# A fused two-layer convolution kernel: gate and NCA in batches of 32 rows, the gate's products over 2 sources x 6 rows in the lattice's column order, NCA's part of two blocks at once

## The chip, the cores and the metric

The kernel runs on one core of a Trainium2 chip. A core has five engines that run beside each other, each with its own instruction stream: TensorE (PE, matmuls, with its weight loads listed as PEld), VectorE (DVE), ScalarE (ACT), GpSimd (POOL) and SyncE (SP), which here issues nearly all DMAs. TensorE's array has 128 x 128 cells; a matmul may use half or a quarter of its columns (or half of its rows), and matmuls on different parts can run side by side. The metric is device time in microseconds (us), from runs of the whole program; the profile is of one execution.

## The reference, cut to what matters

The input is 32 images of 8 channels, 256 x 256, float32. Layer 0 normalises each pair of channels (`_gn`) and then computes three things and mixes them:

```python
drive = x[:, :C_OUT]; grid = drive
for _ in range(STEPS):                       # 15 steps: the lattice (CML)
    mapped = R * grid * (1.0 - grid)
    local = _conv(mapped, K_local, groups=C_OUT)          # 3x3, per channel
    physics = (1.0 - EPS) * mapped + EPS * local
    grid = (1.0 - BETA) * physics + BETA * drive
cml_out = jnp.clip(grid, 0.0001, 1.0 - 0.0001)
h = jax.nn.relu(_conv(x, Wp, bp))            # NCA: 3x3, 8 -> 128
nca_out = jax.nn.sigmoid(_conv(h, Wu, bu))   # 1x1, 128 -> 8
gin = jnp.concatenate([x, cml_out, nca_out], axis=1)      # 24 channels
g = jax.nn.sigmoid(_conv(jax.nn.relu(_conv(gin, Wg1, bg1)), Wg2, bg2))  # gate: 3x3, 24 -> 8; 1x1, 8 -> 8
return g * cml_out + (1.0 - g) * nca_out
```

Here `x` is the normalised input; the layer's result is added to the input. Layer 1 normalises that sum, quantises it with one scale over all images, convolves it (3x3, 8 to 8) and adds again.

## The kernel before, in words

The kernel has two stages. The first is layer 0 for all images, the second layer 1. The images go in 8 groups (NG) of 4 (GB). Work passes between the parts through scratch in HBM: `xp_s` (normalised input in rows with padding, as a high and a low part), `xq_s` (normalised input with its columns sorted into four phases, column 4j+q at place 64q+j), `cm_s` (CML, in the same column order), `nc_s` (NCA, plain columns) and `y_s` (layer 0's result). `xp_s`, `xq_s`, `cm_s` and `nc_s` have 12 buffers of an image each (NBUF).

Four parts share the engines in the first stage.

- *prep* (`normalise`): takes jobs of one image and one or two channel pairs, has the statistics summed by two small matmuls (L330, L359), and stores to `xq_s` and `xp_s`.
- *lattice*: 8 channels x 15 steps a group. A step has three tiles of columns; each tile runs six matmuls (L511), in array halves, for two halves of the group (`jobs`), then two VectorE operations each (L519, L524). After a step, rows at tile borders are exchanged by DMAs on SP (`exchange`, L474 and L475). `background` (L464) spreads the loads of the next channel and the stores of the last over the steps, three DMAs a tile.
- *nca*: `rows` (L569) loads windows of 48 partitions (6 rows of 8 values: three input rows, high and low part) for 28 rows of an image in two parts. `hidden` (L591) runs pairs of matmuls in two halves of the array's rows, ScalarE applies Relu (L601), and `place` (L608) sums 128 hidden values to 8 outputs with matmuls of 32 array columns, up to four side by side. A tenth batch has the last 4 rows.
- *gate*: 9 batches of 28 rows and one of 4, an image. A batch is two blocks of 16 rows x 8 channels on 128 partitions, which overlap by two rows, since a block of 16 rows gives 14. `stage` loads `nb`, `cq` and `xb` (the raw input) with DMAs on SP. `arrange` puts CML's columns back in order on GpSimd (L723), normalises `xb` on VectorE into `xnb` (L729), and forms `d` and `f` on GpSimd. Then 9 matmuls in two array halves (L795), three sources x three column shifts, 512 columns each, then Relu (L812), the second matmul (`pg`, L758), Sigmoid (L760), mix and statistics (L762 to L773), and a store.

The order of TensorE's instructions is the order in which the program writes them (`manual_schedule`). It is set by generators: `lattice` is the main one; `together` lets it do a step (it yields 5.91) and then takes pieces from the filler until the filler's share done equals the lattice's. The filler is made by `both` from nca of the group, gate of the group before, and prep of the next. The shares are reckoned with `T_NCA, T_GATE, T_PREP, T_LATTICE` (L916) and with the numbers that the generators yield, which are the author's guesses of a piece's time. The gate of the last group runs after the last lattice, alone. SP issues its DMAs in the program's order too, and an issue that waits holds all behind it.

In the second stage (from L936) `yb` is loaded from `y_s`, quantised, convolved and stored, image by image.

Of the kernel before, what the change touches and what calls it, by code (L numbers as in the profile page):

```python
# [40 lines left out]
P = 128  # L41
C = 8
# [11 lines left out]
ROW = 2 * C * PW  # L54
R4 = 32
# [12 lines left out]
K_M, K_A, K_B, K_MASK, K_JUNK, K_GRP = 0, 384, 512, 640, 644, 646  # L68
K_COLS = 650


def _constants():
# [5 lines left out]
    n = 2 * H * W  # L78
    same = (c[:, None] // 2) == (c[None, :] // 2)
    mask_a = (r >= 1) & (r <= 14)  # L80
    mask_b = (r >= 1) & (r <= 4)
    k[:, K_A : K_A + P] = same * mask_a[:, None] * (18.0 * W / n)
    k[:, K_B : K_B + P] = same * mask_b[:, None] * (1.0 * W / n)
    k[:, K_MASK + 0] = mask_a
    k[:, K_MASK + 1] = mask_b
    k[:, K_MASK + 2] = r >= 1
    k[:, K_MASK + 3] = r <= 4
# [26 lines left out]
def kernel(  # L114
# [26 lines left out]
    masks = cp.tile([P, 4], F32, name="masks")  # L141
    sel_a = cp.tile([P, P], F32, name="sel_a")
    sel_b = cp.tile([P, P], F32, name="sel_b")
# [7 lines left out]
    gw = cp.tile([P, 9, P], F32, name="gw")  # L151
# [16 lines left out]
    xq_s = [dp.tile([C, H, 4, NJ], F32, name=f"xq_s{i}") for i in range(NBUF)]  # L168
    cm_s = [dp.tile([PROWS, C, W], F32, name=f"cm_s{i}") for i in range(NBUF)]
    nc_s = [dp.tile([PROWS, C, W], F32, name=f"nc_s{i}") for i in range(NBUF)]  # L170
    y_s = [dp.tile([PROWS, C, W], F32, name=f"y_s{b}") for b in range(B)]

    with tc.tile_pool(name="prep", bufs=1) as pp, tc.tile_pool(name="prep2", bufs=2) as pp2:
# [5 lines left out]
        g1 = pp.tile([P, 216], F32, name="g1")  # L179
        nc.sync.dma_start(g1, wg1)  # L180
# [17 lines left out]
        for t, n, w in (  # L198
            *((t, 2 * C, PW) for t in xp_s),
            *((t, C, W) for t in (*nc_s[:GB], *cm_s[:GB], *nc_s[GB:], *cm_s[GB:], *y_s)),  # L200
        ):
            k = 64 if w == W else 43
            for row, m in ((0, 1), (257, 5), (262, 5), (267, 1)):
                borders.append(
                    (
                        dram_ap(t, row * n * w, [[w, m * n], [k, w // k], [1, k]]),
                        zt[: m * n, :k].unsqueeze(1).to_broadcast([m * n, w // k, k]),
                    )
                )
        for _ in range(4 * GB):  # L210
            nc.scalar.dma_start(*borders.pop(0))

        V.tensor_copy(masks, kt[:, K_MASK : K_MASK + 4])
        V.tensor_copy(junk, kt[:, K_JUNK : K_JUNK + 2])
        V.tensor_copy(grp, kt[:, K_GRP : K_GRP + 4])
        V.tensor_copy(sel_a, kt[:, K_A : K_A + P])
        V.tensor_copy(sel_b, kt[:, K_B : K_B + P])
# [22 lines left out]
        for s in range(3):  # L240
            for dx in range(3):
                blocks(gw[:, s * 3 + dx, :], g1, lambda dy: ((s * 3 + dy) * 3 + dx) * C)
# [23 lines left out]
    with ExitStack() as one:  # L266
# [7 lines left out]
        hp, xp, sp2, gp, bp2 = pool("hp", 12), pool("xp", 4), pool("sp2", 1), pool("gp", 3), pool("bp2", 2)  # L274
        st, imp, wk, wk1, np_ = pool("st", 2), pool("imp", 3), pool("wk", 2), pool("wk1", 2), pool("np", 1)
        ps_c, ps_a = pool("ps_c", 6, space=PSUM), pool("ps_a", 2, space=PSUM)
# [3 lines left out]
        xnbs = [fixed([P, 2, PW], f"xnb{i}") for i in range(2)]  # L280
        cmbs = [fixed([P, 2, PW], f"cmb{i}") for i in range(3)]
        nbs = [fixed([P, 2, PW], f"nb{i}") for i in range(3)]
# [3 lines left out]
        for t in (*xnbs, *cmbs, *nbs):  # L286
            for w in (0, PW - 1):
                G.memset(t[:, :, w], 0.0)
# [12 lines left out]
        def normalise(jobs):  # L301
# [36 lines left out]
            def stores(b, g, xq):  # L338
                for h in range(2):
                    nc.sync.dma_start(  # L340
                        dram_ap(xq_s[b % NBUF], (2 * g * H + P * h) * W, [[W, P], [H * W, 2], [1, W]]),
# [54 lines left out]
        def lattice(g):  # L396


            def load(u):
# [4 lines left out]
                for s in range(2):  # L404
                    i = (2 * u + s) % 4
                    da, db = d_a[i], d_b[i]
                    for k in range(2):
                        src = xq_s[((u // C) * GB + 2 * s + k) % NBUF]
                        ts = slice(NT * k, NT * k + NT)
                        for i in range(8):  # L410
                            q, odd = divmod(i, 2)
                            dims = [[2 * W, 16], [TSTEP * W, NT], [1, NJ]]
# [168 lines left out]
        def nca(b):  # L581
# [85 lines left out]
            if done:  # L667
                nc.sync.dma_start(*done)
# [427 lines left out]
```

## Time and profile before

| | |
|---|---|
| time before, median of 3 runs | 13897.23 us (13894.44 to 13898.17) |
| span of the profiled execution | 13862.1 us |
| median less that span | 35.1 us |
| instructions | 229831 |
| granted TensorE clock, mean | 0.975 |
| DMA packets | 2287210, 1496.77 MB, mean 108 GB/s |
| lattice matmuls (L511) | 2 x 17280 instructions |
| nca matmuls (L591; L608) | 2 x 12288; 8320 |
| gate matmuls (L795; L758) | 3 x 3840; 1280 |
| first lattice matmul, last | 86 us, 12930 us |
| last gate matmul | 13291 us |

The profile gives, for every engine, when each instruction ran. "Busy" is the time in which an engine ran anything; a busy TensorE is not TensorE at its peak, since its matmuls are pipelined and overlap. What a stream of matmuls costs is read from the distance between starts. The chain of waits follows the program back from its last instruction, at each step to what released it, so that its shares say what the span was spent on. A float32 matmul shows as two instructions (two passes), each with a weight load. Group 0's lattice has nca but no gate beside it, groups 1 to 7 have both.

### The profile page before, as it was taken

Reading aid. Unit: us, or ns where it says so; the run is one execution under the profiler, and the core shown is the slowest. Engines: PE = TensorE matmul, PEld = TensorE weight load, DVE = VectorE, ACT = ScalarE, POOL = GpSimd, SP = SyncE. Lnnn points to the kernel's source line nnn. Section 1 sums busy time; section 2 is a strip of 40 time slices with the busy share of each in tenths; the row PEclk is TensorE's granted clock in tenths of the full one; section 3 lists DMA queues with packets and bytes.
Section 4 is the critical chain, followed back from the end, with each engine's and each line's share of the span. In section 5 each row is a group of like instructions: output and inputs, shape, how many; then the busy total and the mean of one; then the engine's idle time right before and its main releaser. Section 6 shows DMA issues by size and latency. Waiting matters only on the chain.

```text
span 13862.1 us, 229831 instructions
## 1 busy us (share of the span) xinstructions
PE 13134.4 (95%) x81840; PEld 6403.4 (46%) x81840; DVE 8176.8 (59%) x16402; ACT 4028.2 (29%) x6274; POOL 2454.7 (18%) x4278
## 2 busy tenths in 40 slices
PE   4899999999999999999999999999999999999964
PEld 2445544444444444444444444444444444444322
DVE  5555565566655565555655565555655555555577
ACT  2233223232322223322323223222223222222123
POOL 1001111121111211111111111112111111111310
PEclk8999999999999999999999999999999999999986
DMA  6444444444444444444444444444444433333368
GB/s 152 96 97 99 96 104 112 101 98 101 111 99 103 109 93 108 108 104 93 107 106 101 102 104 103 102 106 108 94 108 110 100 91 84 89 79 89 90 202 257
DMA packets 2287210, 1496.77 MB, mean 108 GB/s; under 512 B 1096576, under 2 KB 2257152, under 8 KB 2285952
## 3 DMA queue, kind: packets, MB, share of 16 engines
q1 hardware_dynamic: 2191360, 1392.13, 43.1%
q10 hardware_dynamic: 94720, 89.93, 2.1%
q8 instruction: 665, 10.90, 0.3%
q14 instruction: 465, 3.81, 0.1%
HBM read 866.48 MB, written 478.69 MB: 97 GB/s over the span
## 4 chain that ended last, share of the span: by engine, by line
PE 81%; DMA 8%; SPq 4%; DVE 3%; issue 1%; ACTq 1%; ACT 0%; POOL 0%; POOLq 0%; DVEq 0%
PE pt L511 36%; PE ph L591 20%; PE pa L795 16%; PE acc L608 7%; DMA yb<-y_s 2%; PE pg L758 2%; DMA im<-xp_s 1%; DVE gt L519 1%; ACTq L1021 1%; DMA m_a<-m_a 1%; DMA xb<-in_x_dram 1%; DMA xp_s<-lo 1%; SPq L464 1%; SPq L569 1%; DVE m_a L524 1%
## 5 line engine op out<-in xcount | busy, mean ns | idle before, releaser
L511 PE MATMUL pt<-m_a,lw 128*64 128x390 f32 x17280 | 5842.6, 496 | 162.0 <-DMA m_a<-m_a 103.3
L511 PE MATMUL pt<-m_b,lw 128*64 128x384 f32 x17280 | 5809.7, 491 | 18.9 <-DVE m_b L430 18.1
L601 ACT ACTIVATE h<-ph,bp_sb 128x512 f32<-128x512 f32 x4096 | 2581.8, 684 | 4845.8 <-PE ph L591 4772.4
L511 PEld LDWEIGHTS pt<-m_a,lw 128*64 128x64 f32 x17280 | 2302.2, 138 | 1795.4 <-issue 1597.2
L511 PEld LDWEIGHTS pt<-m_b,lw 128*64 128x64 f32 x17280 | 2310.1, 138 | 1638.4 <-issue 1522.3
L591 PE MATMUL ph<-im,wp_hi 48*128 48x512 f32 x12288 | 2685.1, 415 | 119.0 <-DMA im<-xp_s 59.4
L519 DVE SCALAR_TENSOR_TENSOR gt<-pt,d_b 128x390 f32<-128x390 f32 x2880 | 1609.3, 559 | 1820.8 <-PE pt L511 1818.2
L519 DVE SCALAR_TENSOR_TENSOR gt<-pt,d_a 128x384 f32<-128x384 f32 x2880 | 1584.1, 550 | 1837.4 <-PE pt L511 1836.7
L591 PE MATMUL ph<-im,wp_lo 48*128 48x512 f32 x12288 | 2569.9, 398 | 0.0
L528 POOL TENSOR_TENSOR m_b<-m_b,junk 128x12 f32<-128x12 f32 x2688 | 817.1, 304 | 8414.1 <-DVE m_b L524 7988.0
L591 PEld LDWEIGHTS ph<-im,wp_hi 48*128 48x128 f32 x12288 | 1312.0, 187 | 969.7 <-DVE m_a L524 180.7
L524 DVE SCALAR_TENSOR_TENSOR m_b<-gt 128x390 f32<-128x390 f32 x2688 | 1557.1, 579 | 46.4 <-DVE gt L519 0.9
L524 DVE SCALAR_TENSOR_TENSOR m_a<-gt 128x384 f32<-128x384 f32 x2688 | 1540.3, 573 | 18.0
L591 PEld LDWEIGHTS ph<-im,wp_lo 48*128 48x128 f32 x12288 | 1309.2, 188 | 218.6
L608 PE MATMUL acc<-h,wu_z 128*32 128x512 f32 x8320 | 1155.1, 598 | 6.1 <-ACT nca L626 5.5
L795 PE MATMUL pa<-cmb,gw 128*64 128x512 f32 (+1 forms) x3840 | 861.4, 580 | 15.5 <-POOL cmb L723 15.5
L795 PE MATMUL pa<-xnb,gw 128*64 128x512 f32 (+1 forms) x3840 | 847.8, 574 | 11.1 <-ACT r L812 11.1
L795 PE MATMUL pa<-nb,gw 128*64 128x512 f32 (+1 forms) x3840 | 847.2, 573 | 0.0
L762 DVE TENSOR_TENSOR gate<-gate,d 128x512 f32<-128x512 f32 x320 | 218.3, 682 | 823.0 <-ACT gate L760 805.0
L812 ACT ACTIVATE r<-pa,bv 128x512 f32<-128x512 f32 x320 | 213.1, 666 | 1650.4 <-PE pa L795 1650.4
L729 DVE TENSOR_SCALAR xnb<-xb,sc 128x256 f32<-128x256 f32 x608 | 305.0, 517 | 596.9 <-DMA xb<-in_x_dram 590.7
L760 ACT ACTIVATE gate<-pg,bv 128x512 f32<-128x512 f32 x320 | 213.2, 666 | 1519.1 <-PE pg L758 1508.1
(133 smaller groups left out, 7225.3 us busy)
## 6 DMA issues: line engine op xcount, KB each, us to landing
im<-xp_s SPq DMA_DIRECT2D x1152, 193.5 KB
im<-xp_s SPq DMA_DIRECT2D x1216, 96.8 KB
d_a<-xq_s SPq DMA_DIRECT2D x2048, 36.0 KB
nb<-nc_s SPq DMA_DIRECT2D x288, 256.0 KB
cq<-cm_s SPq DMA_DIRECT2D x288, 256.0 KB
xb<-in_x_dram SPq DMA_DIRECT2D x544, 128.0 KB
yb<-y_s ACTq DMA_DIRECT2D x28, 2432.0 KB
xp_s<-hi SPq DMA_DIRECT2D x256, 258.0 KB
```

What stands on the lines that cost most here:

```text
L511: T.matmul(pt[half], lw[:, c, k, half], beside if part == 2 else own, start=part < 2, stop=part > 0,)
L519: V.scalar_tensor_tensor(gt, pt, FLOOR, d[:, ts, :], ALU.max, ALU.add)
L524: V.scalar_tensor_tensor(to, gt, 1.0, gt, ALU.subtract, ALU.mult)
L528: G.tensor_tensor(edge, edge, junk.unsqueeze(1).to_broadcast([P, 6, 2]), ALU.mult)
L591: T.matmul(ph[:, :n].rearrange("p (h w) -> p h w", w=W), w[64 * i : 64 * i + 48, dx, :], rhs[:, :, dx : dx + W], start=(dx == 0 and w is w ...
L601: S.activation(h[:, :n], ph[:, :n], AF.Relu, bias=bp_sb)
L608: T.matmul(acc[32 * g : 32 * g + 32, :cols], wu_z[:, 24 - 8 * i : 56 - 8 * i], h, start=first, stop=last,)
L729: V.tensor_scalar(xnb[:, k, 1 : 1 + W], xb[:, k, :], sc[:, i : i + 1], sc[:, 1:2], ALU.subtract, ALU.mult,)
L758: T.matmul(pg[half, :cols], gw2[:, half], r1[:, :cols], start=True, stop=True)
L760: S.activation(gt[:, :cols], pg[:, :cols], AF.Sigmoid, bias=bv[:, 1:2])
L762: V.tensor_tensor(three(y), three(gt), d[:, :n, :], ALU.mult)
L795: T.matmul(three[half], gw[:, s * 3 + dx, half], t[:, :n, dx : dx + W], start=(i == 0), stop=(i == 8),)
```

## The change

Gate and nca now work in 8 batches of 32 rows, an image, with nothing left over. All three sources of the gate lie in one scratch tensor `gs_s` of three parts (normalised input, CML, NCA), all in the lattice's column order; `xq_s` goes, and the lattice loads from part 0. NCA's Sigmoid (ScalarE) writes its columns in that order. The gate loads `gin` (96 partitions: 6 rows x 8 channels of the normalised input and of CML; 8 blocks of 4 output rows), `gnc` (96 partitions: twice 6 rows of NCA, for two blocks) and `mix` (the three sources at the output rows). A block of 4 rows gives 32 outputs, so one matmul over `gin` has 32 array columns, and one over `gnc` 64. A column shift in the sorted order is a move by 64 places, except at a phase border, so each shift but the middle one falls into two pieces (`PARTS`).

```diff
-    xq_s = [dp.tile([C, H, 4, NJ], F32, name=f"xq_s{i}") for i in range(NBUF)]
-    cm_s = [dp.tile([PROWS, C, W], F32, name=f"cm_s{i}") for i in range(NBUF)]
-    nc_s = [dp.tile([PROWS, C, W], F32, name=f"nc_s{i}") for i in range(NBUF)]
+    gs_s = [dp.tile([3, PROWS, C, W], F32, name=f"gs_s{i}") for i in range(NBUF)]
...
-        for _ in range(4 * GB):
+        for _ in range(2 * NBUF):
             nc.scalar.dma_start(*borders.pop(0))
...
-        hp, xp, sp2, gp, bp2 = pool("hp", 12), pool("xp", 4), pool("sp2", 1), pool("gp", 3), pool("bp2", 2)
-        st, imp, wk, wk1, np_ = pool("st", 2), pool("imp", 3), pool("wk", 2), pool("wk1", 2), pool("np", 1)
-        ps_c, ps_a = pool("ps_c", 6, space=PSUM), pool("ps_a", 2, space=PSUM)
+        hp, xp, sp2, gp, gip = pool("hp", 8), pool("xp", 3), pool("sp2", 1), pool("gp", 3), pool("gip", 2)
+        st, imp, wk, np_ = pool("st", 2), pool("imp", 2), pool("wk", 2), pool("np", 1)
+        ps_c, ps_a = pool("ps_c", 6, space=PSUM), pool("ps_a", 1, space=PSUM)
...
+        def rows(b, t):
+
+            im = imp.tile([P, 2, 8, PW], F32R, name="im", tag="im")
+            for k in range(2):
                 for q in range(2):
                     nc.sync.dma_start(
+                        im.bitcast(F32)[64 * q : 64 * q + 48, k],
+                        dram_ap(
+                            xp_s[b % NBUF], (32 * t + 16 * k + 8 * q) * ROW, [[PW, 48], [ROW, 8], [1, PW]]
+                        ),
                     )
...
+            def drain():
+                acc, t, i, hs = pend
+                for g in range(4):
+                    T.matmul(
+                        acc[32 * g : 32 * g + 32], wu_z[:, 24 - 8 * i : 56 - 8 * i], hs[4 * g + i],
+                        start=(i == 0), stop=(i == 3),
+                    )
...
+            for t in range(NT8):
+                im = ahead
+                acc = ps_a.tile([P, 512], F32, name="acc", tag="acc")
+                for i in range(4):
                     hs = {}
+                    for n in (i, i + 4):
+                        hs[n], hs[n + 8] = hidden([im[64 * q : 64 * q + 48, :, n, :] for q in range(2)])
+                    if i == 2:
...
+                        if t < NT8 - 1:
+                            ahead = rows(b, t + 1)
...
+                    if pend:
+                        done = drain() or done
+                    pend = (acc, t, i, hs)
+                    yield 3.7
...
+        def stage(b, t):
+
+            src = gs_s[b % NBUF]
+            gin = gip.tile([96, 8, W], F32, name="gin", tag="gin")
+            for j in range(2):
                 nc.sync.dma_start(
+                    gin[48 * j : 48 * j + 48],
+                    dram_ap(src, j * PART + 32 * t * C * W, [[W, 48], [4 * C * W, 8], [1, W]]),
                 )
+            gnc = gip.tile([96, 4, W], F32, name="gnc", tag="gnc")
+            for h in range(2):
+                nc.sync.dma_start(
+                    gnc[48 * h : 48 * h + 48],
+                    dram_ap(src, 2 * PART + (32 * t + 4 * h) * C * W, [[W, 48], [8 * C * W, 4], [1, W]]),
                 )
+            mix = gip.tile([P, 3, 2, W], F32, name="mix", tag="mix")
+            for k in range(2):
+                nc.sync.dma_start(
+                    mix[:, :, k, :],
+                    dram_ap(src, (32 * t + 16 * k + 1) * C * W, [[W, P], [PART, 3], [1, W]]),
                 )
...
+        def arrange(sc, mix):
+
+            d = wk.tile([P, 512], F32, name="d", tag="d", bufs=1)
+            f = wk.tile([P, 512], F32, name="f", tag="f", bufs=1)
+            G.tensor_tensor(d, flat(mix[:, 1]), flat(mix[:, 2]), ALU.subtract)
+            S.activation(f, flat(mix[:, 0]), AF.Identity, bias=sc[:, 0:1], scale=sc[:, 2:3])
+            G.tensor_tensor(f, f, flat(mix[:, 2]), ALU.add)
+            return d, f
...
+        PARTS = (
+            (1, slice(0, 256), slice(0, 256)),
+            (0, slice(64, 256), slice(0, 192)),
+            (0, slice(1, 64), slice(192, 255)),
+            (2, slice(0, 192), slice(64, 256)),
+            (2, slice(192, 255), slice(1, 64)),
+        )
...
+            for t in range(NT8):
+                gin, gnc, mix = ahead
+                pa = ps_a.tile([P, 512], F32, name="pa", tag="pa")
+                three = pa.rearrange("p (k w) -> p k w", w=W)
+                for n, (dx, to, of) in enumerate(PARTS):
+                    for i in range(4):
+                        T.matmul(
+                            three[32 * i : 32 * i + 32, :, to], gw[:, dx, :32], gin[:, i::4, of],
+                            start=(n == 0), stop=False,
+                        )
+                if last:
+                    if done:
+                        nc.sync.dma_start(*done)
+                    done = finish(*last)
+                yield 2.6 + 0.9 * bool(last)
+                for n, (dx, to, of) in enumerate(PARTS):
+                    for i in range(2):
+                        T.matmul(
+                            three[64 * i : 64 * i + 64, :, to], gw[:, dx, 32:], gnc[:, i::2, of],
+                            start=False, stop=(n == len(PARTS) - 1),
+                        )
+                r1 = wk.tile([P, 512], F32, name="r1", tag="r1", bufs=1)
+                S.activation(r1, pa, AF.Relu, bias=bv[:, 0:1])
+                last = (t, r1, *arrange(sc, mix))
+                if t < NT8 - 1:
+                    ahead = stage(b, t + 1)
...
-        def prep(g, groups=((0, 1), (2, 3))):
+        def prep(g, groups=((0,), (1,), (2,), (3,))):
...
-        T_NCA, T_GATE, T_PREP, T_LATTICE = 520.0, 340.0, 34.0, 8 * 45 * 1.97
+        T_NCA, T_GATE, T_PREP, T_LATTICE = 520.0, 158.0, 34.0, 8 * 45 * 1.97
```

`finish` runs the second matmul in four array quarters instead of two halves, mixes, and writes `y` with its columns back in plain order on VectorE; it is otherwise as before. The sums behind layer 1's statistics need one set of batch statistics instead of two (full and last batch). The zero borders written to scratch at the start are fewer rows of `xp_s` and of `gs_s`. The gate's weight blocks are built on the host (`wg1`) instead of on VectorE.

## The prediction

> **What bounds the kernel now.** I read the page's busy times and its chain first, then the TensorE timeline of a stretch in the middle, then the table of windows.
>
> ```profile
> PE 13134.4 (95%) x81840; PEld 6403.4 (46%) x81840; DVE 8176.8 (59%) x16402; ACT 4028.2 (29%) x6274; POOL 2454.7 (18%) x4278
> ...
> PE pt L511 36%; PE ph L591 20%; PE pa L795 16%; PE acc L608 7%; DMA yb<-y_s 2%; PE pg L758 2%; DMA im<-xp_s 1%; DVE gt L519 1%; ACTq L1021 1%; DMA m_a<-m_a 1%; DMA xb<-in_x_dram 1%; DMA xp_s<-lo 1%; SPq L464 1%; SPq L569 1%; DVE m_a L524 1%
> ```
>
> TensorE is busy for 95% of the span and the chain stands on it for 81%. The gate's share is pa and pg, 18%. So matmul time removed is time won, where TensorE stays the last one. What a matmul costs is read from starts, not from durations, since matmuls overlap (columns: start, length, what, count):
>
> ```profile
> 6002.31 2.80 PE L795 MATMUL pa<-xnb,gw 128*64 128x512 f32 x12
> 6004.94 1.03 PE L758 MATMUL pg<-r,gw 128*64 128x512 f32 x4
> 6005.79 0.49 PE L511 MATMUL pt<-m_a,lw 128*64 128x390 f32 x1
> ...
> 6011.33 0.49 PE L511 MATMUL pt<-m_a,lw 128*64 128x390 f32 x1
> 6011.75 0.50 PE L591 MATMUL ph<-im,wp_hi 48*128 48x512 f32 x2
> ...
> 6014.85 1.92 PE L608 MATMUL acc<-h,wu_z 128*32 128x512 f32 x16
> 6016.71 2.80 PE L795 MATMUL pa<-cmb,gw 128*64 128x512 f32 x12
> 6019.33 0.49 PE L511 MATMUL pt<-m_a,lw 128*64 128x390 f32 x1
> ```
>
> A float32 matmul is two instructions. The gate's 12 (2 column halves side by side, so 6 rounds) take 6004.94 - 6002.31 = 2.63 us, and pg's 2 rounds 0.85: **0.43 us a round of 512 columns**. acc's 16 instructions use 32 columns of the array each and take 1.86 us: four side by side, 4 rounds of 0.43 and a little. So a quarter-width matmul costs a quarter. A change of array shape (6011.33 to 6011.75, where lattice rounds follow at 0.32) costs 0.10.
>
> ```profile
> 13035.14 1.46 PE L795 MATMUL pa<-xnb,gw 128*64 128x256 f32 x12
> ...
> 13036.43 1.03 PE L758 MATMUL pg<-r,gw 128*64 128x512 f32 x4
> ...
> 13055.00 0.38 PE L830 MATMUL pm<-ma,sel_a 128*128 128x1 f32 x2
> ...
> 13055.24 0.36 PE L831 MATMUL pm<-mb,sel_b 128*128 128x1 f32 x2
> ```
>
> With 256 columns 6 rounds take 1.29, 0.215 each: cost goes with columns. The last two rows are the smallest matmuls there are: 0.24 for two, 0.12 each, one after the other over the whole array.
>
> ```profile
> core 0: us, PE busy (x) PEld busy (x) DVE busy (x) ACT busy (x) POOL busy (x), PEclk, DMA share, GB/s
> ...
> 6000.00:8000.00 2000.00, 1971.18 (x12420) 957.66 (x12418) 1186.60 (x2451) 587.80 (x918) 378.84 (x647) 0.99 0.45 103
> ...
> 13000.00:13100.00 100.00, 99.37 (x486) 34.67 (x484) 50.22 (x110) 16.07 (x24) 47.33 (x49) 1.00 0.37 112
> ...
> 13500.00:13862.00 362.00, 174.88 (x666) 80.41 (x665) 282.23 (x181) 138.19 (x210) 0.00 (x0) 0.69 0.82 258
> ```
>
> Middle and gate-only tail are TensorE's at full clock; layer 1 (the last row) is the DMA's. By the last NCA activation of each image (L676) group 0 ends at 1595 us, and a group of 1 to 6 takes 1620. The lattice ends at 12930, the gate of group 7 runs alone to 13291.
>
> I summed rounds for 3300 to 4900 us from all matmul starts: lattice 688, hidden 355 (0.235 a pair), acc 108, gate 326, small 8, together 1486 of 1600; 337 changes of shape at 0.096 make 32; 82 are waits. I also took each lattice step's period less the other work in it: 6.1 to 6.9 us wherever 2 us or more of other work lies in it, however much, and 8.4 in the 5 steps without any. So the lattice does not need the gate as cover, only some.
>
> **The change, part by part.**
>
> Gate matmuls. Before, an image has 9 batches of 18 + 2 rounds at 0.43 and one of 20 at 0.215: 81.7 us. After, a batch has 5 pieces of 512, 384, 126, 384, 126 columns, in two passes: 2 x (0.43 + 2 x 0.3225 + 2 x 0.106) = 2.57 us. x and CML together run it once, in quarter-width matmuls four side by side as acc does; NCA once more, two side by side; pg's four quarters take 0.86. That is 6.0 a batch, 48 an image, 33.7 less; **134 a group of four images**.
>
> Not shown in the trace is a round of 126 columns. Bounds: 0.106 by columns, and every instruction at 0.12 alone, 0.48 for a round of four and 0.24 for two, which adds 4 x 0.37 + 4 x 0.13 = 2.0 us a batch, 64 a group. I take 0.115 (nearest row: 256 columns without any fixed cost): 2 a group.
>
> The Trainium skill's TensorE: Matmul & The Clock Gate, section Back-to-back issue gap, speaks against this step: a stream of weight load and matmul pairs of 128 columns is said to hold about 81 ns a matmul. By it the 24 narrow matmuls of a batch would take 1.94 us, not 0.85, and the whole time would be some 240 us above my sum. acc's quarter matmuls at 1.86 us for 16 (116 ns each, with 512 columns) do not decide it.
>
> Prep by single channel pairs: 8 more jobs a group, each with two small sums on TensorE at about 0.4 (two rows of 0.12 and the change of shape): 6.6 a group. Their VectorE work, 8 x 1.2 by the rows of L323 to L361, lies beside TensorE.
>
> Shape changes. NCA drains once per step of i (32 an image, before 19), and the gate now has a quarter-width and a half-width part. I count 60 more a group, 6 us; bounds 0 and 15.
>
> Filler that runs out. NCA yields 477 a group, gate 155, prep 48: 680 where the planner's times say 712, so the last 4.5%, 5 to 6 steps of a lattice, stand bare at 8.4 instead of 6.8. Before it was 886 of 894, one step. 7 us more.
>
> So a group of 1 to 7 wins 134 - 2 - 6.6 - 6 - 7 = 112: **784**.
>
> Removed at nothing: VectorE's xnb (L729, 305 us) and GpSimd's copies (L723, 410 us) lie beside TensorE. VectorE waits at xnb for xb's DMA 591 us, in order ahead of the lattice, but the chain has 1% on that; 0 to 18 a group, I take 0. ScalarE gains 256 x 0.69 for f; it is at 29%.
>
> Loads. A batch brings gin 768 KB, gnc 384, mix 768, 15.7 MB an image against 7.3; NCA's im comes as 1.55 MB at once:
>
> ```profile
> im<-xp_s SPq DMA_DIRECT2D x1152, 193.5 KB
> ...
> nb<-nc_s SPq DMA_DIRECT2D x288, 256.0 KB
> cq<-cm_s SPq DMA_DIRECT2D x288, 256.0 KB
> xb<-in_x_dram SPq DMA_DIRECT2D x544, 128.0 KB
> ```
>
> In the middle the DMA share goes from 0.45 to about 0.55. The lattice's exchange (L474) shares SP's queue, but a batch's loads are issued behind a step's exchange, and the next comes a step later. I take nothing; see the rivals.
>
> The tail, 361 us now. TensorE would need 32 x (6.0 + 1.0), as pa has one buffer now and waits for r (0.69 and the handover): 225. The transfers, 32 x 2.23 MB, take 235 at 303 GB/s (112 over a share of 0.37) and 270 at the 264 GB/s reached in layer 1. DMA becomes last; with the first load and the last chain 285: **76** won, bounds 20 and 130.
>
> Group 0 has no gate, yet loses 151 of 990 us (600 to 1590) to waits, 15% against 5%. SP issues there for 1060 of 1490 us: 433 loads of im (208 us) and 217 zero fills (162). im's become 128, the zero fills 200. I take a third of the excess of some 150 over the group: **50**, bounds 0 and 130.
>
> Sum: 13862 - 784 - 76 - 50 = 12952. The median of the runs shown, 13897, lies 35 above the span; so **12987**.
>
> **The rivals.**
> 1. Larger gain (0.13): group 0 loses as little as the others (130), xb's waits count (15 x 7), the tail is TensorE's (130). Then 12987 - 80 - 105 - 54 = 12750 at most, 12830 in the middle. For it: SP's load there; against: the chain's 1% on xb.
> 2. Narrow rounds dear (0.14): up to 64 a group in 7 groups, 448, to 13435; 13220 in the middle. For it: 8 instructions (4 weight loads) must start in 0.106 us. Against: 256 columns at no fixed cost.
> 3. The change does not do what it says (0.04): with 96 rows the quarters do not run four side by side but two; 2.57 more a batch, 82 a group, 575: 13560. Against it: acc, four side by side over 128 rows.
> 4. Slower (0.05): bursts hold the exchange. Per group 32 of im (5.2 us at 300 GB/s) and 32 of the gate (6.6). The gain of 910 is gone from 910 / 448 bursts = 2.0 us each; if half a burst (3 us) counts, 7 x 64 x 3 = 1344: 14330. For it: one queue in order, m_a in the chain. Against: TensorE waits for m_a only 103 us in all, beside bursts of 0.77 MB.
> No change (0.02) lies between 3 and 4.
>
> **How the numbers follow.** The forecast has 0.62, within 12890 to 13110 (tail and group 0 at their bounds). Range 12800 to 13300: it leaves out the lower end of 1, the upper third of 2, and 3 and 4, about 0.18. 0.2% of the time, 28 us, is what measurement can tell from none. Faster 0.93, same 0.02, slower 0.05.
>
> **What would show it.** In the changed profile: gate rounds by starts, 6.0 us a batch; narrow rounds at 0.11; a group's period 1508; a tail near 285 with a DMA share above 0.8; five bare steps at a group's end; in group 0 fewer waits; TensorE still 95%. Wrong if TensorE waits for m_a or im by hundreds of us, or if quarter-width rounds come later than their columns allow.

## The result: slower by 3.1%

| | before | after |
|---|---|---|
| time, median | 13897.7 us, 4 runs (13894.4 to 13908.1) | 14337.4 us, 4 runs (14334.7 to 14349.6) |
| ratio | | 1.0314 [1.0299, 1.0328] |
| span | 13862.1 us | 14332.9 us |
| granted clock, mean | 0.975 | 0.928 |

The forecast was 12987 us and faster. The page of the changed kernel, busy times and three groups of matmuls (busy, mean ns, then idle time ahead and what ended it):

```profile
PE 12513.1 (87%) x86432; PEld 6325.1 (44%) x86432; DVE 7785.2 (54%) x15344; ACT 4092.9 (29%) x6338; POOL 1969.4 (14%) x3522
...
L498 PE MATMUL pt<-m_a,lw 128*64 128x390 f32 x17280 | 5936.2, 512 | 543.9 <-DMA m_a<-m_a 498.8
...
L722 PE MATMUL pa<-gin,gw 96*32 96x384 f32 (+2 forms) x10240 | 830.4, 477 | 352.7 <-DMA gin<-gs_s 282.4
...
L733 PE MATMUL pa<-gnc,gw 96*64 96x384 f32 (+2 forms) x5120 | 714.0, 424 | 0.0
```

TensorE is busy 87% of the span, not 95%, and its idle time now has DMAs behind it. (The chain of waits on this page breaks off after 8% on TensorE and can't be read; so what follows goes by TensorE's own waits.) They are, first before and then after (us in total, times, longest):

```profile
PE pt L511 <- DMA m_a<-m_a: 103.3, 71, 8.2
PE ph L591 <- DMA im<-xp_s: 59.4, 31, 26.2
PE pm L330 <- DVE mv L323: 58.2, 4, 35.0
```

```profile
PE pt L498 <- DMA m_a<-m_a: 498.8, 176, 8.8
PE pa L722 <- DMA gin<-gs_s: 282.4, 41, 24.3
PE pm L313 <- DVE mv L306: 263.3, 34, 14.6
...
PE ph L562 <- DMA im<-xp_s: 118.7, 44, 20.0
PE pv L346 <- DVE e L318: 116.3, 42, 8.4
```

Three waits have grown: on the lattice's exchange (m_a), on the gate's load (gin), and on prep's sums (mv and e, which VectorE forms from xr's load). Cut into stages at the first lattice matmul of each group, the two spans differ by 471 us, 1381 from the forecast of 12952:

| us | before | forecast | after |
|---|---|---|---|
| up to group 0's lattice | 86 | 86 | 67 |
| group 0 | 1541 | 1491 | 1640 |
| groups 1 to 6, each | 1620 | 1508 | 1686 |
| group 7 | 1585 | 1473 | 1570 |
| gate alone (tail) | 361 | 285 | 361 |
| the rest | 571 | 571 | 577 |

1071 of the 1381 lie in groups 1 to 6. There TensorE waits 987 us in all six together (before 130), m_a 366 of them, gin 226, prep 270, im 44, and the clock has a mean of 0.942 (0.994). Where a text below or a recorded expectation says what m_a is "a group" or "in the groups after the first", these sums over six groups are meant.

One such wait, SP's DMA issues in the changed kernel (start, length):

```profile
7740.04 1.22 SPq L611 DMA_DIRECT2D gs_s<-nca  x1
7741.32 2.39 SPq L543 DMA_DIRECT2D im<-xp_s  x4
7743.92 0.62 SPq L461 DMA_DIRECT2D m_a<-m_a  x1
7744.58 0.61 SPq L462 DMA_DIRECT2D m_a<-m_a  x1
7746.46 0.56 SPq L461 DMA_DIRECT2D m_a<-m_a  x1
7747.06 0.56 SPq L462 DMA_DIRECT2D m_a<-m_a  x1
7747.67 2.83 SPq L640 DMA_DIRECT2D gin<-gs_s  x2
7752.79 2.67 SPq L646 DMA_DIRECT2D gnc<-gs_s  x2
```

and TensorE in the same stretch:

```profile
7743.56 0.49 PE L498 MATMUL pt<-m_a,lw 128*64 128x390 f32 x1
7743.85 0.49 PE L498 MATMUL pt<-m_b,lw 128*64 128x384 f32 x1
7743.89 0.49 PE L498 MATMUL pt<-m_a,lw 128*64 128x390 f32 x1
...
7747.28 1.06 PE L581 MATMUL acc<-h,wu_z 128*32 128x512 f32 x8
7756.31 0.88 PE L498 MATMUL pt<-m_a,lw 128*64 128x390 f32 x1 [7.96 <-DMA m_a<-m_a]
...
7756.98 0.86 PE L498 MATMUL pt<-m_a,lw 128*64 128x390 f32 x1
...
7761.44 0.49 PE L498 MATMUL pt<-m_a,lw 128*64 128x390 f32 x1
7761.71 0.49 PE L498 MATMUL pt<-m_b,lw 128*64 128x384 f32 x1
7761.77 0.49 PE L498 MATMUL pt<-m_a,lw 128*64 128x390 f32 x1
```

The four loads of im (1.55 MB) go out directly ahead of two exchanges of two transfers of 16.5 KB each. TensorE waits for the first of these exchanges: VectorE wrote its rows by 7743.84, so it is issued without delay, at 7743.92 and 7744.58. But here the transfers land in the order of their issue. By their semaphores the four loads land at 7747.60, 7750.18, 7752.77 and 7755.15, the exchange only then, at 7755.61 and 7756.17, 11 us after its issue, and TensorE starts at 7756.31. In that time the granted clock falls to 0.5 (from 7751.02 on). This is a second price: lattice rounds start 0.67 us apart (7756.31, 7756.98) where they started 0.33 apart before the wait, until the clock is back at 7761.26.

Is this the rule? In groups 1 to 6 TensorE waits for m_a for more than 1.5 us at 85 places, 335 us in all. At 77 of them, 315 us, a load of im is among the eight issues of SP ahead of the exchange that it waits for; of all exchange transfers, a quarter have one there. And of the 127 exchange transfers in the run that directly follow a load of im, 101 land after it.

For all 1344 exchanges of groups 1 to 6 I took two distances from the trace: from the end of VectorE's write of the rows to the end of the exchange's two issues ("issued late"; the two issues alone take 1.2 us), and from there to the landing of its second transfer ("lands late"):

| | issued after write, mean us | landed after issue, mean us | landings over 5 us |
|---|---|---|---|
| before | 1.75 | 1.34 | 1 |
| after | 2.21 | 1.87 | 103 |
| im's loads spread (e3) | 2.13 | 1.71 | 49 |
| exchange on ScalarE's queue (e6) | 1.26 | 2.49 | 165 |
| one list (e8) | 2.04 | 1.84 | 14 |
| one list, lattice's own loads slower (e9) | 1.66 | 1.65 | 7 |
| one list, ScalarE's queue (e10) | 1.26 | 2.15 | 50 |
| no loads (e11) | 1.46 | 1.29 | 0 |
| small loads (e12) | 1.42 | 1.27 | 0 |

The expectations of e9 and e10 speak of 3.2, 2.2 and 0.6 us. Those were taken over the waits above 1.5 us alone. By the semaphores TensorE often waits for an earlier exchange than the last one issued, as at 7756.31; so the readings below go by all exchanges, as in the table.

### The profile page after: what moved, and what is told of

The parts are those of the page before. It is cut to its first block, busy times and chain, and to the rows that moved or that the text cites. A ratio compares the mean times of both kernels' runs of the same rounds, so it can differ in the third digit from the quotient of the medians.

```text
span 14332.9 us, 234662 instructions
## 1 busy us (share of the span) xinstructions
PE 12513.1 (87%) x86432; PEld 6325.1 (44%) x86432; DVE 7785.2 (54%) x15344; ACT 4092.9 (29%) x6338; POOL 1969.4 (14%) x3522
## 5 line engine op out<-in xcount | busy, mean ns | idle before, releaser
L498 PE MATMUL pt<-m_a,lw 128*64 128x390 f32 x17280 | 5936.2, 512 | 543.9 <-DMA m_a<-m_a 498.8
L498 PE MATMUL pt<-m_b,lw 128*64 128x384 f32 x17280 | 5882.8, 505 | 18.9 <-DVE m_b L417 18.6
L511 DVE SCALAR_TENSOR_TENSOR m_a<-gt 128x384 f32<-128x384 f32 x2688 | 1500.2, 558 | 19.6
L722 PE MATMUL pa<-gin,gw 96*32 96x384 f32 (+2 forms) x10240 | 830.4, 477 | 352.7 <-DMA gin<-gs_s 282.4
L581 PE MATMUL acc<-h,wu_z 128*32 128x512 f32 x8192 | 1113.8, 616 | 3.4 <-ACT nca L587 3.4
L695 DVE TENSOR_TENSOR gate<-gate,d 128x512 f32<-128x512 f32 x256 | 178.3, 696 | 1135.0 <-ACT gate L694 1135.0
L722 PEld LDWEIGHTS pa<-gin,gw 96*32 96x32 f32 x10240 | 342.5, 121 | 892.8 <-issue 774.0
L733 PE MATMUL pa<-gnc,gw 96*64 96x384 f32 (+2 forms) x5120 | 714.0, 424 | 0.0
L664 POOL TENSOR_TENSOR d<-mix 128x512 f32<-128x512 f32 x256 | 471.2, 1841 | 1575.5 <-DVE gate L695 1276.9
L733 PEld LDWEIGHTS pa<-gnc,gw 96*64 96x64 f32 x5120 | 360.4, 137 | 439.7 <-issue 406.9
```

The source lines that it names most:

```text
L498: T.matmul(pt[half], lw[:, c, k, half], beside if part == 2 else own, start=part < 2, stop=part > 0,)
L511: V.scalar_tensor_tensor(to, gt, 1.0, gt, ALU.subtract, ALU.mult)
L581: T.matmul(acc[32 * g : 32 * g + 32], wu_z[:, 24 - 8 * i : 56 - 8 * i], hs[4 * g + i], start=(i == 0), stop=(i == 3),)
L664: G.tensor_tensor(d, flat(mix[:, 1]), flat(mix[:, 2]), ALU.subtract)
L695: V.tensor_tensor(gt, gt, d, ALU.mult)
L722: T.matmul(three[32 * i : 32 * i + 32, :, to], gw[:, dx, :32], gin[:, i::4, of], start=(n == 0), stop=False,)
```

## The experiments

**Theories.** A: bursts of loads stand ahead of the lattice's exchange, as rival 4 had it. B: the gate's loads are asked for too late. C: the list of steps is drawn up with wrong sums. D: the bytes as such are too many, however spread. Against all: the new matmuls themselves are dearer (rivals 2 and 3). Gain below is against 14337 us; "group" is the mean period of groups 1 to 6. e8, e9 and e10 are medians of four runs, the others one run each; the kernel before beside them took 13898 to 13907 us.

| | time, us | gain | group | m_a | gin | prep |
|---|---|---|---|---|---|---|
| after | 14337 | | 1686 | 366 | 226 | 270 |
| e1 gate's loads asked for earlier | 14165 | 172 | 1661 | 490 | 0 | 274 |
| e2 measured sums | 13994 | 343 | 1638 | 370 | 198 | 0 |
| e3 im's loads spread | 13827 | 510 | 1628 | 224 | 200 | 274 |
| e4 gate's loads for one batch of eight | 13656 | 681 | 1586 | 214 | 0 | 266 |
| e5 f twice | 14281 | 56 | 1685 | 353 | 226 | 270 |
| e6 exchange on ScalarE's queue | 14211 | 127 | 1668 | 249 | 136 | 240 |
| e7 = e1 + e2 + e3 | 13594 | 743 | 1603 | 511 | 0 | 0 |
| e8 one list for all loads | 13290 | 1047 | 1562 | 262 | 0 | 0 |
| e9 = e8, lattice's own loads slower | 13964 | 373 | 1659 | 259 | 47 | 0 |
| e10 = e8 + e6 | 14043 | 295 | 1664 | 188 | 24 | 0 |
| e11 e2, no loads | 12738 | 1600 | 1485 | 46 | 0 | 0 |
| e12 small loads | 13163 | 1175 | 1540 | 82 | 0 | 275 |

### e1: gate's loads asked for earlier

```diff
+                if t < NT8 - 1:
+                    ahead = stage(b, t + 1)
+                elif (b + 1) % GB:
+                    staged[b + 1] = begin_gate(b + 1)
                 yield 2.6 + 0.9 * bool(last)
...
-                if t < NT8 - 1:
-                    ahead = stage(b, t + 1)
-                elif (b + 1) % GB:
-                    staged[b + 1] = begin_gate(b + 1)
```

> The changed kernel with the gate's loads for the next batch issued one piece earlier (before the gate's second part instead of after it). In groups 1 to 6 of the changed kernel TensorE stands 226 us on gin's DMA, 366 on m_a's, 270 on prep's two small sums, 44 on im's. Theory B (the gate's loads are issued one NCA step before they are needed): the waits on gin fall below 30, those on m_a and prep stay, the time falls by 200 to 280, to 14060 to 14140. Theory D (it is the volume of DMA, 0.58 of its engines, that slows every transfer): gin's waits stay above 150, or move to m_a, and the time stays within 60 of 14337.

The waits on gin are gone, and m_a rises from 366 to 490, the longest from 8.8 to 17.1 us. So B is right for gin, but the burst only moved to another exchange: of the waits over 1.5 us on m_a, those with a load of the gate (and none of im) shortly ahead rise from 12 to 92 us. The run gains 172 us where 200 to 280 were expected.

### e2: the sums of the list of steps

```diff
-        T_NCA, T_GATE, T_PREP, T_LATTICE = 520.0, 158.0, 34.0, 8 * 45 * 1.97
+        T_NCA, T_GATE, T_PREP, T_LATTICE = 478.0, 163.0, 48.0, 8 * 45 * 1.97
```

> The changed kernel with the planner's three shares set to the sums that the generators really yield (NCA 478, gate 163, prep 48, instead of 520, 158, 34). Theory C (prep yields 48 where 34 was planned, so that five or six of its jobs run one after the other at each group's end, each waiting for its own load): TensorE's waits on prep's two sums fall from 270 us to below 80 in groups 1 to 6, and the time falls by 200 to 300, to about 14090. Theory D (volume): prep's loads are late wherever they stand; waits stay above 180 and the time within 60 of 14337.

The new numbers are what the generators really yield. With prep at 34, its last jobs are left for the end of a group, where they run one after the other, each waiting for its own load. All 270 us of that are gone and a group takes 48 us less; m_a does not move (370). C is a cause by itself. (The gain, 343 us, is above the 200 to 300 expected; group 0 has 70 of it.)

### e3: im's loads spread

```diff
-                        if t < NT8 - 1:
-                            ahead = rows(b, t + 1)
...
+                    if dmas and i < 3:
+                        for _ in range(2 if i == 2 else 1):
+                            nc.sync.dma_start(*dmas.pop(0))
```

> The changed kernel with NCA's four loads of a batch (1.55 MB) issued over three of the batch's four steps (1, 1, 2) instead of all in one; same bytes, same number of DMAs. Theory A (a burst of loads that SP issues just ahead of the lattice's exchange holds the exchange): waits on m_a fall from 366 us to 180 to 260 in groups 1 to 6 (the gate's bursts of 1.97 MB remain), the time falls by 100 to 250, to about 14160. Theory D (volume): waits on m_a stay above 320, time within 60 of 14337.

Same bytes, same queue, one or two loads at a time: m_a falls to 224, as expected, and landings over 5 us from 103 to 49. The run gains 510 us, twice what was expected, and is 72 us below the kernel before (one run each). Part of the surplus is the clock: the slow clock (granted 0.5) costs TensorE's busy time 39 us a group in place of 59. Bytes alone (D) can't explain that.

### e4: gate's loads for one batch of eight

```diff
-        def stage(b, t):
+        def stage(b, t, kept=[]):
+            if t:
+                return kept[0]
```

> The changed kernel with the gate's loads made for the first batch of each image only; the other seven batches reuse them, so the gate's values of those are left out (those of batch 0 stand in their place). It takes 13.8 of 15.7 MB an image away and no other work. Theories A, B, C: gin's waits go (226 to under 40), m_a's fall to about half (im's bursts remain), prep's stay (270), the tail falls from 361 us to 240 to 290 (TensorE's); time 13750 to 13950. Theory D (volume): prep's and im's waits fall too, to under a third, and the time goes to 13500 or less.

m_a falls to 214, as with e3, and the run to 13656, some 100 us below what A to C expected: both bursts, im's and gate's, cost time. The tail, which has hardly any loads here, still takes 351 us, so it is not held by its transfers.

### e5: two buffers for f

```diff
-            f = wk.tile([P, 512], F32, name="f", tag="f", bufs=1)
+            f = wk.tile([P, 512], F32, name="f", tag="f", bufs=2)
```

> f, the buffer that takes gate's sigmoid, gets two buffers in place of one; nothing else is touched. In the last image's gate, which runs alone, the groups after the change show TensorE waiting 55 us in 25 places for ScalarE's r, and ScalarE waits for VectorE's y, the reader of the one f. If the order on ScalarE sets that stage, the waits on r fall below 15 us and the stage from 361 us to 240 to 290, the whole run to 14220 to 14270 us. If the stage is held by its transfers, as the prediction had it, it stays at 340 us or more and the run at 14320 to 14345. Among the steps nothing should move by either.

The tail of the changed kernel, on three engines:

```profile
13519.23 2.18 DVE L697 TENSOR_TENSOR y<-gate,f 128x512 f32<-128x512 f32 x1
...
13521.44 0.81 ACT L665 ACTIVATE f<-mix,sc 128x512 f32<-128x512 f32 x1 [3.10 <-DVE y L697]
...
13522.16 0.67 ACT L738 ACTIVATE r<-pa,bv 128x512 f32<-128x512 f32 x1
...
13522.88 4.48 PE L722 MATMUL pa<-gin,gw 96*32 96x512 f32 x40 [2.25 <-ACT r L738]
```

ScalarE has f ahead of r in its stream, f waits for y's read of the one buffer, and TensorE waits for r; its 40 matmuls then take 4.5 us, at a granted clock of 0.5 (13522.95 to 13526.37), in place of 2.6. With two buffers the waits on r fall from 55 to 12 us and the tail from 361 to 313, less than expected: gin's transfers come next (waits on gin in the tail 60 us in place of 38, DMA share 0.86 in place of 0.76). The window of 13300 to 13700, first in the changed kernel, then in e5:

```profile
13300.00:13700.00 400.00, 295.42 (x2346) 127.04 (x2350) 189.79 (x312) 61.34 (x88) 84.51 (x85) 0.84 0.76 171
```

```profile
13300.00:13700.00 400.00, 311.74 (x2680) 138.08 (x2684) 193.93 (x339) 74.28 (x104) 114.07 (x96) 0.88 0.86 197
```

### e6: the exchange on another queue

```diff
-                nc.sync.dma_start(t[0::16, below, :], t[14::16, above, :])
-                nc.sync.dma_start(t[15::16, above, :], t[1::16, below, :])
+                nc.scalar.dma_start(t[0::16, below, :], t[14::16, above, :])
+                nc.scalar.dma_start(t[15::16, above, :], t[1::16, below, :])
```

> The two transfers of a step that exchange rows between the lattice's parts are issued from ScalarE's queue in place of SP's; all other transfers stay where they are. If it is the order in SP's one queue (an exchange issued just behind four of im's loads or three of gate's), TensorE's waits for m_a in the groups after the first fall from 366 us a group of four images to under 120, and the run to 13900 to 14150 us; a price against it is ScalarE, whose other work waits while its queue stands before an exchange that waits for VectorE's m_a. If it is the load on the DMA engines themselves, whatever queue a transfer is in, m_a stays over 300 and the run within 60 us of 14337.

Neither number: m_a is 249. By the table above, the late issue is gone (2.21 to 1.26 us, little more than the issues themselves), the late landing is not: it grows (1.87 to 2.49). The wait has two parts, and the other queue takes away one. ScalarE pays for it: TensorE's waits on r rise from 15 to 108 us in the six groups. The Trainium skill's DMA: Bandwidth & Descriptors, section Issuing engines are not separate DMA queues, says that DMAs started by different engines run on the same 16 DMA engines and interleave; that the exchange lands no sooner from the other queue (2.49 us, 1.87 before the move) agrees.

### e7: e1, e2 and e3 together

> The three edits that were run alone together: gate's loads for a batch issued behind phase 1 of the batch before (14165 alone), the sums by which the list of steps is drawn up set to the measured ones (13994), and im's four loads spread over three steps in place of one (13827). If their causes are apart, the gains of 172, 343 and 510 us add up: 13310, in 13230 to 13400. If they share a cause (fewer slow-clock stretches, or one burst that takes the other's place, as gate's loads did when im's were left in one burst), the sum is less, 13450 to 13650, and m_a keeps over 200 us a group.

743 of 1025 us: the causes overlap. m_a is highest here (511). Of the waits over 1.5 us (474 us), 392 have a load of the gate shortly ahead of the exchange, where it was 33 of 335 in the changed kernel: gate's six loads now stand in one burst, as in e1.

### e8: all loads through one list

```diff
             def background(n):
+                if soon:
+                    nc.sync.dma_start(*soon.pop(0)[1:])
...
-                    nc.sync.dma_start(
+                    soon.append(("im",
                         im.bitcast(F32)[64 * q : 64 * q + 48, k],
```

(The same for gin, gnc and mix; what is left is issued when its batch begins. With e1's place, e2's sums and e5's buffer.)

> All loads of im and of gate go through one list, from which one is issued behind the exchange of each step's tile, so two a step; gate's loads are asked for behind phase 1; the sums of the list of steps are the measured ones; f has two buffers. By the theory of bursts ahead of the exchange, m_a falls to under 80 us a group, gin, im and the waits on prep together to under 60, and the last gate to 240 to 290 us: 13000 to 13200 us, faster than both kernels. By the theory that the bytes alone load the DMA engines, m_a stays over 200 and the run over 13350.

13290.4 us, ratio to before 0.9564 [0.9548, 0.9580]: faster than both kernels, with every byte of the change. (Not by the list alone: e2's sums and e5's buffer, both apart from the loads, have their part in it.)

```profile
PE pt L501 <- DMA m_a<-m_a: 340.0, 238, 6.1
...
PE pa L735 <- DMA gin<-gs_s: 68.5, 18, 25.5
PE ph L571 <- DMA im<-xp_s: 51.9, 12, 20.6
```

The time is 90 us above what A expected. m_a did not fall under 80; over the run it is many short waits now (238, 1.4 us each; landings over 5 us are down from 103 to 14), the clock in groups 1 to 6 is 0.982, and the tail takes 320 us, with gin's transfers last. Theory D would have m_a over 200, which it is, and the run over 13350, which it isn't.

### e9: fewer of the lattice's own transfers behind a tile

```diff
-                        background(3)
+                        background(1)
```

> The kernel of the smooth list, with one of the lattice's own loads and stores issued behind each tile in place of three. In the smooth kernel the waits on m_a over 1.5 us have two parts: the exchange goes out 3.2 us after VectorE has written m_a, and TensorE starts 2.2 us after that. If the first part is the issuing itself (six descriptors of some 0.6 us between two exchanges), it falls to about 1 us, m_a from 262 to 120 to 180 us in the groups after the first, and the run to 13120 to 13220 us. If the first part is a wait for an earlier transfer that has not landed, it stays and the run is within 50 us of 13290. Against it: the stores of the last step come later, so the steps after a group's end may run bare for longer.

Ratio to before 1.0043 [1.0028, 1.0058]: 674 us slower than e8. A miss, by a wait that had been looked for only at a group's end:

```profile
PE pt L501 <- DVE m_b L418: 585.5, 58, 18.3
PE pt L501 <- DMA m_a<-m_a: 279.9, 126, 135.4
```

m_b of L418 is the start of the next channel; it reads d_b, which is copied from d_a and now arrives too late, at nearly every channel. (Without one wait of 135 us, m_a is at 124 in the six groups, as low as expected, and the exchange is issued 1.66 us after the write in place of 2.04: so a part of e8's late issue comes from the lattice's own transfers.)

### e10: e8 with the exchange on ScalarE's queue

> The kernel of the smooth list with the exchange issued from ScalarE's queue. With the one burst gone, the late issue should go too (it fell from 3.2 to 0.6 us when the exchange alone was moved), while the 2.2 us to the start stays: m_a from 262 to 100 to 150 us, the run to 13100 to 13200 if ScalarE's other work, which then waits behind VectorE's m_a, costs TensorE nothing. If TensorE's waits on ScalarE (r, h) rise by what m_a gives back, as a third of it was lost when the exchange alone was moved, the run stays at 13250 to 13330.

Ratio to before 1.0105 [1.0088, 1.0122]: 752 us slower than e8, by neither of the ways expected. m_a falls to 188, but im is late by 459 us in the six groups, and SP's own waits say why:

```profile
SPq L454 <- DMA m_a<-m_a: 3227.6, 962, 15.2
SPq L452 <- DMA m_a<-m_a: 1465.2, 489, 12.5
```

SP waits before loads of im and gate (L452) for an exchange to land, with which they share no data. In the trace all DMA issues, of SP and of ScalarE, wait for and count up one of the same eight semaphores, used in turn; so SP goes no further than the landing of a transfer some eight issues back, on whichever queue. So the two queues are not independent here.

### e11: no loads, e2's sums

```diff
+            if kept:
+                return kept[0]
```

(ahead of the loads in both `rows` and `stage`)

> The changed kernel with the measured sums in the list of steps, and the loads of im and of gate left out but for the very first batch (NCA and gate work on stale rows; the count of instructions on TensorE is the same). It asks whether the prediction's sum over TensorE's own work was right: 1508 us a group of four images. If the whole loss is in the loads, the groups after the first take 1500 to 1530 us and m_a falls to before's 33 us or less; the run is 12900 to 13050. If the matmuls themselves are dearer than was summed, or the clock is held down by something else, the groups stay over 1560.

A group takes 1485 us, under the 1508 forecast, and the run less than was expected; the clock in groups 1 to 6 is 0.994, and TensorE is busy 95%:

```profile
PE 12103.2 (95%) x86432; PEld 6036.8 (47%) x86432; DVE 7702.5 (60%) x15344; ACT 4099.2 (32%) x6338; POOL 1993.5 (16%) x3522
```

So the matmuls are not dearer than was summed, and the clock is not held down by them. Between this run and e2 only the loads differ: they cost 1638 - 1485 = 153 us a group.

### e12: small loads

```diff
-                        im.bitcast(F32)[64 * q : 64 * q + 48, k],
+                        im.bitcast(F32)[64 * q : 64 * q + 48, k, n:],
...
-                    gin[48 * j : 48 * j + 48],
+                    gin[48 * j : 48 * j + 48, n:],
```

(n is 7 of 8 from the third batch on, with kept buffers; gnc and mix likewise)

> The changed kernel, where each load of im and of gate is still issued, in the same place and from the same queue, but brings only an eighth of im, an eighth of gin, a quarter of gnc and a third of mix (the rest of the rows are stale, from the first two batches). It parts two things that a burst does to the exchange behind it: its bytes on the DMA engines, and its seven or so descriptors in SP's queue. If the bytes do it, also through transfers that have not landed and that SP waits for, m_a falls from 366 us in the groups after the first to under 80, gin's 226 to under 40, and the run to 13700 to 13850, with the waits on prep (270) left. If the issuing does it, m_a stays over 200 and the run over 14050.

The issues stay and the bytes go, and the answer is the bytes (those that stand in bursts, by e3 and e8), with more won than expected: the run is 537 us below the lowest figure named, with m_a at 82. TensorE's waits:

```profile
PE pm L313 <- DVE mv L306: 245.1, 28, 14.9
...
PE pt L498 <- DMA m_a<-m_a: 116.9, 79, 5.9
```

All 13302 issues on SP are still there. Yet the late issue goes too: 1.42 us after the write, as without any load (e11, 1.46), in place of 2.21. So it was no issuing time but SP waiting for transfers that had not landed. In the changed kernel the second of SP's waits is

```profile
SPq L461 <- DVE m_a L511: 4116.0, 1162, 13.6
SPq L451 <- DMA im<-xp_s: 393.8, 243, 3.5
```

L451 issues the lattice's own transfers, which have nothing to do with im. In e12 the same wait is

```profile
SPq L451 <- DMA im<-xp_s: 11.9, 7, 2.3
```

## Why the prediction was wrong

**Gate matmuls (134 us a group): right.** One batch of the changed kernel at full clock:

```profile
5473.76 2.79 PE L722 MATMUL pa<-gin,gw 96*32 96x512 f32 x40
5476.36 1.04 PE L692 MATMUL pg<-r,gw 128*32 128x512 f32 x8
5477.33 0.50 PE L562 MATMUL ph<-im,wp_hi 48*128 48x512 f32 x2
```

40 instructions take 2.60 us with the change to pg, summed at 2.57 without it; pg 0.97 with its change, summed at 0.86. The wide rounds are 2 x (0.43 + 2 x 0.3225) = 2.15, so the four narrow ones have at most 0.45, 0.11 each: the value taken was 0.115. So rivals 2 and 3 did not happen. e11's group, 135 us under before's, has the whole gain.

The Trainium skill's TensorE: Matmul & The Clock Gate, section Back-to-back issue gap (about 81 ns a matmul of 128 columns), would have put the 16 narrow instructions of this part at 1.3 us, an estimate; they took 0.45 at most. It does not hold here for matmuls of 126 columns on quarters of the array side by side.

**Loads ("issued behind a step's exchange, and the next comes a step later. I take nothing"): the step that failed.** SP runs behind: in the timeline above, matmuls that stand after im's loads in the program (acc) ran at 7737.29, and the first load went out at 7741.32. So loads stand directly ahead of the next exchange, and 1.55 MB or more keep the transfers behind them waiting, in landing and, through the eight semaphores, in issuing. A load of im takes 8.4 us from issue to landing on the mean (before 3.7, with half the bytes); the burst above took 13.8 us, where rival 4 had 5.2 by 300 GB/s. The price of all this, put at nothing, is 147 us a group (1686 less e12's 1540; by e2 and e11 153), 147 / 64 = 2.3 us a burst. From the changed kernel to e12 TensorE's waits on the exchange fall by 47 us a group, those on gin and im, which come late themselves, by 45, and the loss to the slow clock by 45.

Rival 4 had named the exchange and the turning point, 2.0 us, and the whole lies just past it. But the waits on the exchange alone are 0.7 us a burst; it is gin, im and the clock, which rival 4 did not have, that carry the price past 2.0. Rival 4 had spoken against itself with m_a's 103 us before, "beside bursts of 0.77 MB"; with twice the burst that became 499.

**Filler that runs out (7 us a group): mis-sized.** The sums were seen to be wrong, 680 yielded where 712 was planned, but read as five bare steps. What is left over for the end is prep, 48 against 34, and its jobs wait for their loads: e2 gives 48 us a group, e12 less e11 54. In steps from e11 over e12 to the changed kernel a group is 1485 + 54 + 147 = 1686; these are differences of the same runs, so the sum by itself proves nothing.

**That the time is rival 4's 14330 is partly chance:** its price was 3 us a burst, measured are 2.3; with the prep jobs' 48 us a group it is (147 + 48) / 64 = 3.05. And rival 4 leaves the tail and group 0 at the forecast, where 76 and 149 us were lost.

**The clock** has no term in the prediction. Waits in groups 1 to 6 rose by (987 - 91) / 6 = 149 us a group over e11, the period by 201. The other 52 are the clock (0.994 to 0.942): the time that TensorE was busy at a granted clock of 0.5, halved, is 59 us a group in the changed kernel and 8 in e11.

**Tail (285 by the transfers): wrong.** 361 stayed, e4 without most loads 351: ScalarE's order set it. With that mended (e5, e8) 313 and 320, where the transfers do come next.

**Group 0 (50 won): wrong, by 149.** It has no gate; im's bursts and the prep jobs met it too (e2 1570, e3 1539, e7 1457 us). That there is something to win in group 0 is not refuted: e8 takes 1460, under the forecast's 1491. Whether fewer issues do it was not tried.

**Open:** e8's group still takes 1562 against e11's 1485. Of these 76 us, 51 are waits (36 on m_a) and 17 the slow clock. Whether they come from the load on the DMA engines however it is spread, or from bursts of the lattice's own transfers, was not parted.

## What to carry to other kernels

Before a change that makes loads larger and fewer, look up which small transfer on the critical path shares the queue or the semaphores, and price each burst by its bytes, not by its issues: here 2.3 us for each burst of 1.55 to 1.97 MB, enough, with the prep jobs, to turn a forecast gain of 6.6% into a loss of 3.1%. The same change with its loads given out one at a time, the planner's sums put right and a second buffer for f is 4.4% faster than before. Where a planner's sums are numbers written by hand, sum what is really yielded, part by part: the total can be nearly right while one part is left for the end. A wait costs more than its length where the clock falls after it.

## What the runs showed of the hardware

- Small transfers mostly land behind the large ones issued ahead of them (101 of 127 directly behind a load of im): 16.5 KB behind four loads of 387 KB landed 11 us after issue, 1.0 us behind the last load. Over groups 1 to 6 the exchange's mean landing is 1.87 us (before 1.34, with small loads 1.27), and moving it to the other queue does not help (2.49).
- Eight semaphores, which this program's DMAs use in turn over both queues, bound how far SP runs ahead: 394 us of waits on im's loads at issues that do not need them, 1465 us before loads in e10.
- In a wait of 8 us the granted clock fell to 0.5 after 2.7 us, and it stayed there for 5 us after the wait (0.67 in place of 0.33 us between rounds).
- Four narrow matmuls (126 columns, float32, a quarter of the array each) take 0.11 us together at most, with their weight loads.
